# A decoder's first layer in one thread: Silu by Tanh, one block's convolution on VectorE, exponentials by tile, four product buffers

## The chip, the cores and the metric

The kernel runs on one core of one Trainium2 chip. The time is that of the device in microseconds (us), from start to end of one execution; less is better. Three runs of the kernel before gave 4592.59, 4599.94 and 4611.69 us, so the median is 4599.94. The profile is one further execution.

The engines are named as in the profile: PE is TensorE, PEld its weight loads, DVE is VectorE, ACT is ScalarE, POOL is GpSimd, SP is the queue that issues DMAs.

## The reference

A decoder of four layers, each with an attention, a cross attention and a feed-forward part, all different, works on x of 8 x 256 x 256 in float32. The change lies in the first of these twelve parts, a selective state space model in both directions. Cut to what matters:

```python
xz = xn @ W_in.T                     # 512 channels u, 512 channels z
u = silu(causal_conv4(u) + b_conv)   # depthwise, 4 taps
for d in (forward, backward):
    dt, Bm, Cm = split(u @ Wx.T)     # 64, 16, 16
    delta = softplus(dt @ Wdt.T + bdt)
    h[t] = exp(delta[t] * A) * h[t-1] + delta[t] * Bm[t] * u[t]   # 16 states
    y_d = sum over states of h[t] * Cm[t] + u * D
out = (y_f + y_b) / 2 * silu(z) @ W_out.T
```

The convolution and its Silu give u, which all else of the layer reads; Silu of z is the gate at its end; the softplus makes the deltas. Silu(v) is v times the logistic function, which is (v/2) * (tanh(v/2) + 1).

## The kernel before

**Two threads.** `build` (from L2480) runs two generators, one for blocks 0 and 1 ("left", the leading thread) and one for blocks 2 and 3 ("right"). A block is two of the eight sequences, 512 positions. Each thread goes through the twelve layers, and every `yield` adds the layer's planned time per step to the thread's clock; the thread that is earlier goes on. The right thread starts with a lag of 1.01 * FIRST = 474.7 planned units, so that the leading thread has its first layer to itself. A layer's planned time is divided by its number of steps, for this one FIRST / WIDE_STEPS = 470 / 265 (L2445). Instructions are then put in order on each engine by a scheduler that starts from this order of emission, and each engine works through its own list in order.

**The leading thread's first layer** is the class `Wide` (L723 on). It works on one block after the other, and on each in two ways, forward and backward. A way has 16 states, each of four tiles of 128 channels x 512 positions, 64 tiles in all. `way` (L782) puts out two tiles of a state, then one step of the parts that belong beside it, and so on.

**A tile** (`state`, L879): ScalarE takes Exp(delta * A) into a bank `st` of PSUM (two banks, L895), POOL multiplies `du` with a row of B that a DMA has spread over the partitions (`db`, four buffers, L897), VectorE runs the scan (L899). For three states of four the result stays in SBUF (`h`, three buffers) and `turn` (L917) transposes it on TensorE into `ht` (two banks), scales it on ScalarE with C (`ys`, L926) and transposes it back, added into y (L929). For the fourth state the result stays in `st`, VectorE multiplies it by the row of C (`hc`, two buffers, L902) and TensorE adds it to y through an identity matrix (L903).

**The parts beside the ways.** `channels` (L796) makes u: norm, transposes, W_in on TensorE, a copy to `u0` on ScalarE with three zero columns in front of each sequence (POOL's memset, L813), the convolution and Silu. In the first block the even channel groups are convolved on VectorE (L819, L821), the odd ones, and all of the next block, as four matmuls with diagonal matrices of taps on TensorE (called at L827, recorded under L395). Silu is L824 or L828. `rows` (L832) projects u to the rows of dt, B and C; `delta` (L852) makes the deltas: Abs (L862), Max (L863), after the last group Exp of -|v| (L867) and Ln (L869) over all four groups at once, sum (L872) and the product with u on POOL (L873). `gates` (L943) makes the Silu of z (L952), `gated` (L955) forms the result (L959, L962). Next block's channels, rows and deltas lie in the backward way of the first block, the second way; the gates lie in the second and the fourth.

A step that yields "ln" asks `way` to hold the next part back until the first half of a state with k % 4 == 3.

Of the kernel before, what the change touches and what calls it, by code (L numbers as in the profile page):

```python
# [8 lines left out]
F32 = mybir.dt.float32  # L9
# [713 lines left out]
class Wide:  # L723
# [8 lines left out]
    def steps(self):  # L732
        net, nc, other = self.net, self.nc, self.other
        with net.scope(y=1), other.scope(st=2, ht=2):
# [15 lines left out]
            nc.vector.tensor_tensor(self.skip, w["fD"], w["bD"], ALU.add)  # L750
            self.turning, last = None, None
# [44 lines left out]
    def channels(self, o, first=False):  # L796
# [12 lines left out]
        for c in range(4):  # L809
# [6 lines left out]
            bias = w["b_conv"][:, c : c + 1]  # L816
            if first and c % 2 == 0:
                acc = self.other.work.tile([128, 2, S], F32, name="hc", bufs=2)
                nc.vector.tensor_scalar(acc, u0[:, :, 0:S], w["conv"][:, c, 0:1], bias, ALU.mult, ALU.add)  # L819
                for k in range(1, 4):  # L820
                    nc.vector.scalar_tensor_tensor(  # L821
                        acc, u0[:, :, k : k + S], w["conv"][:, c, k : k + 1], acc, ALU.mult, ALU.add
                    )
                nc.scalar.activation(u[:, c], acc, AF.Silu)  # L824
            else:
                ps = net.bank()
                net.mms(pairs_of(ps), [(self.taps[:, c, k, :], u0[:, :, k : k + S]) for k in range(4)])  # L827
                nc.scalar.activation(u[:, c], pairs_of(ps), AF.Silu, bias=bias)  # L828
# [23 lines left out]
    def delta(self, o, d, first=False):  # L852
# [5 lines left out]
        for c in range(4):  # L858
            ps = net.bank()
            net.mms(ps, [(w[d + "Wdt"][:64, c * 128 : c * 128 + 128], o["dbc"][d][:64, :])])  # L860
            bias = w[d + "bdt"][:, c : c + 1]
            nc.scalar.activation(du[:, c, :], ps, AF.Abs, bias=bias)  # L862
            nc.vector.tensor_scalar(dl[:, c, :], ps, bias, 0.0, ALU.add, ALU.max)  # L863
            yield "ln" if c == 3 else None
        parts = [du[:, c, :] for c in range(4)] if first else [du]
        for v in parts:
            nc.scalar.activation(v, v, AF.Exp, scale=-1.0)  # L867
        for v in parts:
# [10 lines left out]
    def state(self, o, d, k, half):  # L879
# [12 lines left out]
        for c in (2 * half, 2 * half + 1):  # L892
            with self.net.tc.manual_schedule(engines={mybir.EngineType.Activation}):
# [6 lines left out]
                if not turned:  # L900
                    hc = far.tile([128, 512], F32, name="hc", bufs=2)
# [41 lines left out]
    def gates(self, o):  # L943

        net, nc, w = self.net, self.nc, self.w
        yield "ln"
        res = o["res"] = net.work.tile([128, 4, 512], F32, name="res")
        for c in range(4):
# [3 lines left out]
            nc.scalar.activation(res[:, c, :], ps, AF.Silu)  # L952
        yield

    def gated(self, o):  # L955

        net, nc, u = self.net, self.nc, o["u"]
        for c in range(4):
# [3 lines left out]
            nc.vector.scalar_tensor_tensor(u[:, c], pairs_of(o["res"][:, c, :]), 0.5, u[:, c], ALU.mult, ALU.mult)  # L962
# [1482 lines left out]
FIRST, WIDE_STEPS = 470, 265  # L2445
# [73 lines left out]
```

## Time and profile before

| what | us |
|---|---|
| median of three runs | 4599.94 |
| profiled execution | 4589.32 |
| its span | 4587.5 |
| first scan of the leading thread's first layer (L899) | 48.98 |
| its last hc (L902) | 511.4 |
| VectorE busy from 37 to 511.5 us | 373.0 |
| scans of this layer, 256 | 298.8 |
| ScalarE's Exp of this layer (L895), 256 | 172.2 |
| POOL's db of this layer (L897), 256 | 320.7 |
| table load on ScalarE, each | 1.283 |

How to read it: a row of the profile gives line, engine, operation, the tiles out<-in with their shapes and the number of instructions, then the busy time in us and the mean of one in ns, then how long the engine had been idle just before them and what ended that. A row of a table by stretches gives start and end, the length, and for each engine the busy us and the number of instructions, then the clock that TensorE was granted (1.00 is full), the busy share of the DMA engines and the GB/s. A row of waits gives who waited for whom: us in total, how often, the longest. A row in order of time gives start and length, and in brackets the idle time before it and who ended it. A float32 matmul stands as two records, one for each pass.

### The profile page before, as it was taken

How to read it: one execution, taken by the hardware profiler on the slowest of the kernel's cores; microseconds unless marked ns; L12 is line 12 of the kernel's file. 1: busy time of each engine (PE TensorE's matmuls, PEld its weight loads, DVE VectorE, ACT ScalarE, POOL GpSimd, SP SyncE). 2: the span in 40 equal slices, each digit the busy share in tenths (PEclk: the TensorE clock that was granted, in tenths of full speed). 3: DMA queues.
4: the chain of work that ended last, by engine and by line, in shares of the span. 5: the costliest groups of instructions: out<-in, count | busy, mean ns of one | idle time of the engine just before them, and what ended most of it. 6: DMA issues, size and time to landing. Idle time of an engine off the chain costs nothing.

```text
span 4587.5 us, 55922 instructions
## 1 busy us (share of the span) xinstructions
PE 3953.8 (86%) x20736; PEld 2688.3 (59%) x20736; DVE 2670.8 (58%) x5064; ACT 2028.1 (44%) x4543; POOL 1581.3 (34%) x1373
## 2 busy tenths in 40 slices
PE   6877787887787999989798998798989999978988
PEld 3545444454575767657565665555556768745755
DVE  6768778778656555461665366665474562143464
ACT  6768476677563544423232342423343342243331
POOL 5758445345544111142543233422021001132123
PEclk8999889999898999989899898777799999988999
DMA  3111233234383000017110000100010010011000
GB/s 124 57 36 51 107 92 99 80 77 112 98 266 133 1 1 1 1 45 249 47 42 1 1 33 16 43 14 1 1 49 1 15 37 1 21 41 40 2 37 19
DMA packets 96323, 239.79 MB, mean 52 GB/s; under 512 B 8395, under 2 KB 36403, under 8 KB 85683
## 3 DMA queue, kind: packets, MB, share of 16 engines
q1 hardware_dynamic: 86355, 179.49, 12.5%
q0 software_dynamic: 9696, 56.72, 3.6%
q8 instruction: 164, 2.69, 0.2%
q14 instruction: 108, 0.88, 0.1%
HBM read 216.05 MB, written 20.14 MB: 51 GB/s over the span
## 4 chain that ended last, share of the span: by engine, by line
PE 45%; DVE 13%; POOL 4%; ACT 4%; issue 3%; DMA 2%; POOLq 0%; ACTq 0%; DVEq 0%
PE mm L395 22%; PE sc L403 6%; PE sc L395 5%; PE av L403 3%; PE pt L395 3%; PE o L395 2%; PE mm L1089 2%; DVE xn L418 1%; DMA we<-in_experts,which 1%; PE mm L428 1%; PE mm L403 1%; POOL rs L416 1%; DVE hn_sq L2055 1%; DVE st L411 1%; ACT ex L1475 1%
## 5 line engine op out<-in xcount | busy, mean ns | idle before, releaser
L664 POOL TENSOR_TENSOR db<-du,rep 128x512 f32<-128x512 f32 x256 | 325.0, 1283 | 352.6 <-DVE mm L665 168.7
L665 DVE TENSOR_TENSOR_SCAN mm<-mm,db 128x512 f32<-128x512 f32 x256 | 310.2, 1223 | 92.9 <-ACT mm L662 81.8
L897 POOL TENSOR_TENSOR db<-du,rep 128x512 f32<-128x512 f32 x256 | 320.7, 1283 | 96.3 <-DVE h L899 74.3
L1461 POOL TENSOR_TENSOR qs<-q,w 128x256 f32<-128x256 f32 x256 | 157.6, 636 | 558.4 <-PE sc L395 549.9
L395 PE MATMUL mm<-xt,w 128*128 128x512 f32 (+1 forms) x704 | 302.5, 558 | 30.1 <-DVE rope_s L1412 10.3
L387 ACT COPY pv<-mm 111x384 f32<-111x384 f32 (+2 forms) x388 | 198.0, 512 | 288.9 <-PE mm L1089 128.0
L403 PE MATMUL sc<-k,q 64*128 64x333 f32 (+1 forms) x1152 | 252.3, 491 | 28.2 <-ACT pex L1066 9.8
L395 PE MATMUL sc<-k,qs 128*128 128x256 f32 x1024 | 271.8, 389 | 3.4 <-POOL x L455 1.1
L403 PE MATMUL av<-pv,v 111*64 111x256 f32 (+5 forms) x2752 | 255.2, 388 | 9.3 <-ACT pv L387 5.1
L899 DVE TENSOR_TENSOR_SCAN h<-st,db 128x512 f32<-128x512 f32 x192 | 223.2, 1208 | 43.9 <-ACT st L895 36.7
L395 PE MATMUL mm<-h,sw 128*128 128x256 f32 x1024 | 242.8, 384 | 0.0
L1089 PE MATMUL mm<-consts,pex 128*111 128x128 f32 x960 | 191.9, 310 | 38.1 <-ACT pv L387 30.9
L671 PE MATMUL y<-consts,hc 128*128 128x128 f32 x1024 | 170.9, 295 | 61.3 <-DVE hc L667 60.3
L1089 PEld LDWEIGHTS mm<-consts,pex 128*111 128x111 f32 x960 | 133.0, 185 | 150.0 <-issue 59.9
L395 PE MATMUL mm<-kv,w 128*128 128x256 f32 (+1 forms) x640 | 202.8, 439 | 20.6 <-ACT q L1031 10.4
L395 PE MATMUL mm<-w,ao 128*128 128x256 f32 x768 | 203.6, 405 | 14.2 <-DVE ao L389 5.1
L395 PEld LDWEIGHTS sc<-k,qs 128*128 128x128 f32 x1024 | 183.6, 193 | 49.7 <-issue 21.1
L395 PEld LDWEIGHTS mm<-h,sw 128*128 128x128 f32 x1024 | 192.4, 192 | 32.6 <-issue 6.7
L1475 ACT ACTIVATE ex<-sc,nm 128x256 f32<-128x256 f32 x256 | 119.5, 471 | 196.4 <-DVE nm L1471 182.1
L395 PEld LDWEIGHTS mm<-xt,w 128*128 128x128 f32 x704 | 130.4, 201 | 126.7 <-issue 74.8
L1066 ACT ACTIVATE pex<-sc,pnm 128x333 f32<-128x333 f32 x320 | 170.0, 537 | 76.7 <-DVE pnm L1061 68.5
L403 PEld LDWEIGHTS av<-pv,v 128*32 128x32 f32 (+3 forms) x2752 | 123.2, 133 | 127.9 <-issue 47.0
(484 smaller groups left out, 9098.9 us busy)
## 6 DMA issues: line engine op xcount, KB each, us to landing
rep<-rows2f SPq DMA_DIRECT2D x32, 512.0 KB, 4.8
rep<-rows2b SPq DMA_DIRECT2D x32, 512.0 KB, 4.8
rep<-rows3f SPq DMA_DIRECT2D x32, 512.0 KB, 4.8
rep<-rows3b SPq DMA_DIRECT2D x32, 512.0 KB, 5.2
w<-in_w SPq DMA_DIRECT2D x12, 1024.0 KB, 7.6
w<-in_w SPq DMA_DIRECT2D x8, 1025.0 KB, 9.1
w<-in_w SPq DMA_DIRECT2D x6, 1001.0 KB, 8.3
w<-in_w SPq DMA_DIRECT2D x6, 838.0 KB, 10.9
```

Of the source, the lines that this page charges most:

```text
L387: self.nc.scalar.copy(out, in_)
L395: self.nc.tensor.matmul(out, lhsT=lhs, rhs=rhs, start=n == 0, stop=n == len(pairs) - 1)
L403: self.nc.tensor.matmul(out, lhsT=lhs, rhs=rhs, start=start, stop=stop, tile_position=at)
L664: nc.gpsimd.tensor_tensor(db, du[:, c, :], rep[:, 0], ALU.mult)
L665: nc.vector.tensor_tensor_scan(st[:, order], st[:, order], db[:, order], 0.0, ALU.mult, ALU.add)
L671: nc.tensor.matmul(self.y[i // 2][:, at : at + 128], lhsT=hc[:, i * 128 : i * 128 + 128], rhs=net.ident, is_transpose=True, start=d == "f" ...
L897: nc.gpsimd.tensor_tensor(db, du[:, c, :], self.rep[:, 0], ALU.mult)
L899: nc.vector.tensor_tensor_scan(h[:, order], st[:, order], db[:, order], 0.0, ALU.mult, ALU.add)
L1066: self.nc.scalar.activation(self.ex[:, e, :], self.sc[:, e, :NK], AF.Exp, bias=self.nm[:, e : e + 1], accum_out=self.sm[:, e : e + 1],)
L1089: self.nc.tensor.transpose(pt[:CH, j * 128 : j * 128 + 128], ex[:, e, j * CH : (j + 1) * CH], net.ident)
L1461: nc.gpsimd.tensor_tensor(qs[:, kc].rearrange("p n (h t) -> p n h t", h=H), q[:, kc, t0 : t0 + 16].rearrange("p (n t) -> p n t", n=2).unsq ...
L1475: nc.scalar.activation(ex[:, i, :], sc[:, i * S : (i + 1) * S], AF.Exp, bias=nm[:, i : i + 1], accum_out=sm[:, i : i + 1],)
```

## The change

Silu is taken from Tanh: u becomes (Tanh(v/2) + 1) * (v/2), with v/2 from taps and bias that are halved once at the start (`half`), and the gates become (Tanh(z/2) + 1) * z, which is twice Silu, so that the factor in `gated` goes from 0.5 to 0.25. In the first block's odd groups ScalarE writes v/2 as well. All groups of the next block are convolved on VectorE. The Exp of the deltas follows each group's Abs and Max; only the Ln waits for all four. The gates no longer ask to be held back, and yield after each group. `hc` has four buffers, and the convolution two of its own (`acc`). The constant WIDE_STEPS goes from 265 to 270.

```diff
--- before.py
+++ after.py
@@ -748,6 +748,10 @@
                 nc.vector.tensor_scalar(e, e, -1.0, None, ALU.mult)
                 self.neg_a[d] = e
             nc.vector.tensor_tensor(self.skip, w["fD"], w["bD"], ALU.add)
+
+            self.half = near.tile([128, 5, 4], F32, name="half")
+            nc.vector.tensor_scalar(self.half[:, :4, :], w["conv"], 0.5, None, ALU.mult)
+            nc.vector.tensor_scalar(self.half[:, 4, :], w["b_conv"], 0.5, None, ALU.mult)
             self.turning, last = None, None
             now = {"blk": net.blks[0]}
             for part in (self.channels(now, True), self.rows(now, "f"), self.delta(now, "f", True)):
@@ -813,19 +817,21 @@
             nc.gpsimd.memset(u0[:, :, 0:3], 0.0)
             nc.scalar.copy(u0[:, :, 3:], pairs_of(ps))
             yield
-            bias = w["b_conv"][:, c : c + 1]
-            if first and c % 2 == 0:
-                acc = self.other.work.tile([128, 2, S], F32, name="hc", bufs=2)
-                nc.vector.tensor_scalar(acc, u0[:, :, 0:S], w["conv"][:, c, 0:1], bias, ALU.mult, ALU.add)
+            bias = self.half[:, 4, c : c + 1]
+            acc = near.tile([128, 2, S], F32, name="acc", bufs=2)
+            if not first or c % 2 == 0:
+                nc.vector.tensor_scalar(acc, u0[:, :, 0:S], self.half[:, c, 0:1], bias, ALU.mult, ALU.add)
                 for k in range(1, 4):
                     nc.vector.scalar_tensor_tensor(
-                        acc, u0[:, :, k : k + S], w["conv"][:, c, k : k + 1], acc, ALU.mult, ALU.add
+                        acc, u0[:, :, k : k + S], self.half[:, c, k : k + 1], acc, ALU.mult, ALU.add
                     )
-                nc.scalar.activation(u[:, c], acc, AF.Silu)
+                nc.scalar.activation(u[:, c], acc, AF.Tanh)
             else:
                 ps = net.bank()
                 net.mms(pairs_of(ps), [(self.taps[:, c, k, :], u0[:, :, k : k + S]) for k in range(4)])
-                nc.scalar.activation(u[:, c], pairs_of(ps), AF.Silu, bias=bias)
+                nc.scalar.activation(acc, pairs_of(ps), AF.Identity, scale=0.5, bias=bias)
+                nc.scalar.activation(u[:, c], pairs_of(ps), AF.Tanh, scale=0.5, bias=bias)
+            nc.vector.scalar_tensor_tensor(u[:, c], u[:, c], 1.0, acc, ALU.add, ALU.mult)
             yield
         o["dbc"], o["rows"], o["cols"], o["delta"] = {}, {}, {}, {}
 
@@ -861,11 +867,9 @@
             bias = w[d + "bdt"][:, c : c + 1]
             nc.scalar.activation(du[:, c, :], ps, AF.Abs, bias=bias)
             nc.vector.tensor_scalar(dl[:, c, :], ps, bias, 0.0, ALU.add, ALU.max)
+            nc.scalar.activation(du[:, c, :], du[:, c, :], AF.Exp, scale=-1.0)
             yield "ln" if c == 3 else None
-        parts = [du[:, c, :] for c in range(4)] if first else [du]
-        for v in parts:
-            nc.scalar.activation(v, v, AF.Exp, scale=-1.0)
-        for v in parts:
+        for v in [du[:, c, :] for c in range(4)] if first else [du]:
             nc.scalar.activation(v, v, AF.Ln, bias=1.0)
         yield
         for c in range(4):
@@ -898,7 +902,7 @@
                 h = self.hs[:, c, :] if turned else st
                 nc.vector.tensor_tensor_scan(h[:, order], st[:, order], db[:, order], 0.0, ALU.mult, ALU.add)
                 if not turned:
-                    hc = far.tile([128, 512], F32, name="hc", bufs=2)
+                    hc = far.tile([128, 512], F32, name="hc", bufs=4)
                     nc.vector.tensor_tensor(hc, st, self.rep[:, 1], ALU.mult)
                     nc.tensor.matmul(
                         self.y[c],
@@ -943,14 +947,14 @@
     def gates(self, o):
 
         net, nc, w = self.net, self.nc, self.w
-        yield "ln"
         res = o["res"] = net.work.tile([128, 4, 512], F32, name="res")
         for c in range(4):
             ps = net.bank()
             cols = slice(512 + c * 128, 640 + c * 128)
             net.mms(ps, [(w["W_in"][:, k, cols], o["xt"][:, k, :]) for k in range(2)])
-            nc.scalar.activation(res[:, c, :], ps, AF.Silu)
-        yield
+            nc.scalar.activation(res[:, c, :], ps, AF.Tanh, scale=0.5)
+            nc.vector.scalar_tensor_tensor(res[:, c, :], res[:, c, :], 1.0, ps, ALU.add, ALU.mult)
+            yield
 
     def gated(self, o):
 
@@ -959,7 +963,7 @@
             nc.vector.scalar_tensor_tensor(
                 u[:, c], u[:, c], self.skip[:, c : c + 1], pairs_of(o["y"][c]), ALU.mult, ALU.add
             )
-            nc.vector.scalar_tensor_tensor(u[:, c], pairs_of(o["res"][:, c, :]), 0.5, u[:, c], ALU.mult, ALU.mult)
+            nc.vector.scalar_tensor_tensor(u[:, c], pairs_of(o["res"][:, c, :]), 0.25, u[:, c], ALU.mult, ALU.mult)
         yield
         for b in range(2):
             net.project(o["blk"], b, u[:, :, b], self.w["W_out"])
@@ -2442,7 +2446,7 @@
 SHARE = (620, 300, 150, 300, 80, 140, 140, 120, 170, 110, 160, 100)
 
 
-FIRST, WIDE_STEPS = 470, 265
+FIRST, WIDE_STEPS = 470, 270
 
 
 def steps_of(layer, blks):
```

## Prediction

> **What bounds the kernel now.** I read the page's busy times first, then the busy times of each engine in four stretches of the changed layer, then what VectorE waits for in them, and last the order of time. The page says that TensorE is the busiest engine of the whole program:
>
> ```profile
> PE 3953.8 (86%) x20736; PEld 2688.3 (59%) x20736; DVE 2670.8 (58%) x5064; ACT 2028.1 (44%) x4543; POOL 1581.3 (34%) x1373
> ```
>
> That average says nothing about the leading thread's first layer, which runs nearly alone until 511 us. Its four ways (forward and backward for two blocks) end at 158.6, 299.5, 413.5 and 511.5 us, by the last scan of each:
>
> ```profile
> core 0: us, PE busy (x) PEld busy (x) DVE busy (x) ACT busy (x) POOL busy (x), PEclk, DMA share, GB/s
> 37.00:158.60 121.60, 89.14 (x461) 59.24 (x461) 101.11 (x115) 93.97 (x144) 96.46 (x76) 0.86 0.18 57
> 158.60:299.50 140.90, 110.44 (x517) 67.34 (x516) 91.78 (x94) 100.63 (x146) 85.19 (x71) 0.95 0.13 39
> 299.50:413.50 114.00, 83.41 (x462) 59.41 (x461) 96.27 (x106) 80.51 (x122) 85.80 (x69) 0.93 0.16 47
> 413.50:511.50 98.00, 76.62 (x433) 53.38 (x432) 83.81 (x80) 76.60 (x119) 74.79 (x63) 0.95 0.17 49
> ```
>
> VectorE is idle for 49.1 us of the second way, 17.7 of the third and 14.2 of the fourth. Undisturbed, sixteen state tiles take this:
>
> ```profile
> 391.45:413.45 22.00, 16.36 (x105) 11.63 (x104) 20.86 (x20) 17.48 (x29) 19.77 (x17) 1.00 0.20 61
> ```
>
> VectorE works 20.9 of 22.0 us there: it is the floor, 88 us for a way of 64 tiles, and POOL is close behind at 19.8. So the excess over 88 is either VectorE's other work or waiting. Its waits in the second way:
>
> ```profile
> DVE hc L902 <- PE y L903: 25.3, 3, 12.5
> DVE h L899 <- ACT st L895: 13.0, 11, 3.2
> DVE st L899 <- ACT st L895: 4.1, 5, 1.8
> DVE dl L872 <- ACT du L869: 2.6, 1, 2.6
> ```
>
> Half is one wait: the third product hc needs one of two buffers, freed by TensorE's sum into y. In order of time on VectorE, then on TensorE:
>
> ```profile
> 186.84 1.22 DVE L899 TENSOR_TENSOR_SCAN h<-st,db 128x512 f32<-128x512 f32 x1 [2.67 <-ACT st L895]
> 191.24 1.22 DVE L899 TENSOR_TENSOR_SCAN h<-st,db 128x512 f32<-128x512 f32 x1 [3.18 <-ACT st L895]
> ...
> 219.42 0.69 DVE L902 TENSOR_TENSOR hc<-st,rep 128x512 f32<-128x512 f32 x1 [10.66 <-PE y L903]
> 222.22 0.69 DVE L902 TENSOR_TENSOR hc<-st,rep 128x512 f32<-128x512 f32 x1 [2.10 <-PE y L903]
> ...
> 260.75 0.69 DVE L902 TENSOR_TENSOR hc<-st,rep 128x512 f32<-128x512 f32 x1 [12.50 <-PE y L903]
> ```
>
> ```profile
> 215.78 2.74 PE L395 MATMUL ht<-u,taps 128*128 128x512 f32 x6
> 218.37 1.02 PE L903 MATMUL y<-hc,consts 128*128 128x512 f32 x2
> ```
>
> The sum at 218.37 stands behind the next block's convolution. The waits at 186.84 and 191.24 are ScalarE changing its table for the gates' Silu and back, twice.
>
> **The change, part by part.** The sum is made against the profiled execution: 4589.3 us, of which 4587.5 are the span. The median of the three runs is 4599.9, 10.6 us more; I take the same difference off it.
>
> *Table loads.* These rows, with one shape each, price them:
>
> ```profile
> L895 ACT ACT_TABLE_LOAD x11 | 14.1, 1283 | 0.2
> L952 ACT ACT_TABLE_LOAD x4 | 5.1, 1283 | 0.1
> L872 DVE TENSOR_TENSOR dl<-dl,du 128x512 f32<-128x512 f32 x16 | 15.8, 1016 | 11.9 <-ACT du L869 10.1 <-issue 1.7
> L821 DVE SCALAR_TENSOR_TENSOR hc<-u,w,hc 128x512 f32<-128x512 f32 x6 | 4.5, 747 | 0.1
> L962 DVE SCALAR_TENSOR_TENSOR u<-res,u 128x512 f32<-128x512 f32 x8 | 5.6, 738 | 0.0
> ```
>
> The built order (how the instructions stand on each engine once the kernel is built) has 27 loads in this layer before and 11 after: 16 x 1.283 = 20.5 us of ScalarE time. What counts is what VectorE waited for them. At the gates that is 2.67 + 3.18 + 0.54 = 6.4 us in the second way and 6.4 in the fourth (the same three waits at 441, 446 and 448 us). At the convolution's Silu it is 3.08 + 1.63 at 239 and 246 us. All of it goes: 11.1 us in the second way, 6.4 in the fourth.
>
> *Four buffers and no taps.* The next block's convolution leaves TensorE: 16 instructions, by the trace 3.60 us for a channel group, 14.4 us in all. TensorE then does 110.4 - 14.4 = 96 us of the second way, and VectorE may run two products further ahead. Of 25.3 + 1.75 us (the last is the scan that follows at 263 us) I take 25 off and leave 2: the rows' projections (16 passes in some 7.5 us) still stand in that queue. Bounds: 12 if they alone set the second stall, 27.
>
> *Convolution on VectorE.* Per group one multiply (0.55, L819), three multiply-adds (0.75, L821) and one product for Silu, also 0.75: 3.55 us, 14.2 for four. Here the Trainium skill speaks against the change: by "SBUF — State Buffer", section "Who interferes with whom", a VectorE instruction with two SBUF inputs and a GpSimd one that reads SBUF exclude each other, and the later one blocks until the other is done. The 16 multiply-adds and products have two SBUF inputs, and POOL forms db from two SBUF tiles (1283 ns each) for most of the way. If each had to wait half a db it would cost 16 x 0.64 = 10.3 us more. The nearest row is L872, of the same port pattern beside the same POOL work: it has a mean of 1016 ns with its shortest at 684, so 0.33 each. I take the row: 5.3 us; bounds 0 (L962 has a mean of 738 with POOL idle or waiting) and 10.3.
>
> *New waits.* The product u <- u,acc now waits on VectorE for ScalarE's Tanh, and ScalarE's queue has transposed states in front of it that wait for TensorE. Queued behind it on VectorE are scans and hc, and behind those POOL's db. No row shows this wait; the nearest are the dl waits on ACT at L863, some 0.6 to 3.0 us. The built order puts one to four VectorE instructions between, so I take 0.7 x 4 = 2.8; bounds 0 and 8. POOL's memset of the next padded input now waits for the convolution on VectorE, with db behind it. Before, it waited 8.4 us for the taps matmuls, behind which db lay too. I take 2 us; bounds 0 and 5.
>
> *Gates.* Eight products with one input in PSUM, 0.74 each as the L959 row of that kind: 2.9 us in the second way and 2.9 in the fourth.
>
> *Exponentials by tile.* Four of 0.63 us replace one of 1.9 before the Ln: 0.6 us more of ScalarE, but none of it in one piece in front of the states. At 282 to 299 us VectorE waited 7.4 us round this place; I take 1.4 off it, and 2 off each of ways one and three (there with 3.1 us of hc waits and 5.5 of dl waits).
>
> *Start.* One load less on the chain to the first scan (1.3), two 0.75 us products more on it, partly beside other work: I take -1 in all, bounds -2 and +1. The scaled taps are two VectorE instructions of under 0.2 us, beside the first matmuls: nothing; without that cover 0.4. No DMA is added; of SP's 401 instructions 390 keep their order, so its queue costs nothing here.
>
> Sum for the second way: -11.1 -25.0 -1.4 +14.2 +5.3 +2.8 +2.0 +2.9 = -10.3. Fourth: -6.4 + 2.9 = -3.5. First and third: -4. Start: -1. Together -18.8 us. VectorE after it: 91.8 + 14.2 + 5.3 + 2.9 = 114.2 busy in a way of about 130.
>
> *Behind the layer.* Its steps now number 270, as the constant says; before they were 263 against 265. So the leading thread enters its second layer 3.5 units of planned time later (470 against 466.5), while the other thread still starts at 474.7. From there on the two mix otherwise: of all VectorE's instructions only about 70% stand in a common order. The work is equal, apart from table loads: 158 before, 153 after, and 7 fewer in the trailing thread's state loop (L662), where scans wait for ScalarE. Five are 6.4 us; I take half, -3. The rest I take as nothing. From 520 us on TensorE has 3564 of 4067 us, so 503 idle; a twentieth of that either way is 25 us, an estimate of how far another mixture may move the end.
>
> Total: -21.8, so 4578.
>
> **The rivals.** *A: as summed*, 0.45, at 4578. *B: more of it*, 0.20: the whole 27 us go, no port waits, no Tanh wait, and the later mixture is kinder by 10: -21.8 -2 -5.3 -2.8 -10 = -42, so 4558. For it speaks that TensorE has slack once the taps are gone. *C: the gain doesn't reach the end*, 0.13: VectorE becomes the bound of the second way. With port waits at 10.3, Tanh waits at 8 and the freed stall at 12, the way costs -10.3 + 5.0 + 5.2 + 13.0 = +12.9, hence +1.4 in all: 4601. Against it: POOL itself waits 96 us of the layer. *D: the mixture behind the layer*, 0.22: the trailing thread's state loop (VectorE waits 81.8 us there for ScalarE) and the attentions beside it get in each other's queues; idle TensorE time grows by a tenth, 50 us, less the 21.8: 4628. It decides from about +45 us on. For it: a third of the instructions move. Against it: the work and its steps are the same.
>
> **How the numbers follow.** A measurement tells 0.5%, 23 us: faster is below 4577, slower above 4623. A's spread is about +-12 round 4578, so a bit under half of it counts as faster (0.22) and the rest as same (0.23). B is faster; C is same, with a little to either side; D is slower for the most part. Faster 0.44, same 0.35, slower 0.21. Range: 4546 (B's lower end) to 4625, which leaves most of D out.
>
> **What would show it.** Right: 11 loads before the layer's end; the waits of hc on y gone; the second way near 130 us and the fourth near 94.5; the layer's last scan at about 492 instead of 511; from there to the end within 25 us of the 4076 of before. Wrong: the second way at 140 with multiply-adds of over 1.1 us (C); a layer that ends 20 us earlier with an end that doesn't (D); scans waiting for db behind a memset.

## The result, and the profile after

The changed kernel takes 4624.66 us (median of six runs, 4616.28 to 4627.60) where the kernel before, in the same series, takes 4606.93. The ratio on record is 1.0050, 95% interval 1.0032 to 1.0069 (the two medians alone give 1.0038): slower by about half a per cent. The forecast was 4578, faster by about half a per cent. The sign was wrong; the time lies at the upper end of the range that was given, 4546 to 4625, where rival D stood.

The profiled execution has a span of 4622.0 us against 4587.5. That is 34.5 us more, twice the 17.7 between the medians, since the profiled execution of the kernel before was 17.6 us under its median and that of the changed kernel 0.9. Runs of one kernel differ by some 40 us, the slower ones mostly at a lower clock (51 runs of the kernel before, in a later series, go from 4568.37 us at a mean clock of 0.921 to 4608.19 at 0.910), so a difference of some 10 us between two profiles says little.

The busy times of the whole program, from the page of the changed kernel, say little, and that little is strange: TensorE is busy 24.6 us longer, though it lost the 14.4 us of taps.

```profile
PE 3978.4 (86%) x20704; PEld 2697.1 (58%) x20704; DVE 2708.5 (59%) x5098; ACT 2004.5 (43%) x4533; POOL 1580.7 (34%) x1373
```

The layer itself did what it was meant to. This is the table by stretches of the changed kernel, one row for each way (they end at the last hc of each; start and end, length, then busy time and number of instructions of each engine, granted clock, DMA share, GB/s):

```profile
core 0: us, PE busy (x) PEld busy (x) DVE busy (x) ACT busy (x) POOL busy (x), PEclk, DMA share, GB/s
37.00:161.00 124.00, 92.00 (x461) 61.77 (x462) 101.13 (x115) 93.78 (x145) 95.97 (x76) 0.83 0.18 58
161.00:284.40 123.40, 91.95 (x452) 57.61 (x450) 108.81 (x119) 85.48 (x135) 89.30 (x71) 0.93 0.15 44
284.40:399.70 115.30, 82.02 (x466) 58.92 (x467) 97.45 (x106) 80.48 (x125) 86.54 (x69) 0.94 0.15 46
399.70:498.10 98.40, 74.67 (x449) 53.59 (x448) 85.58 (x84) 72.40 (x116) 75.02 (x61) 0.97 0.16 49
```

The second way fell from 140.9 to 123.4 us, and the layer's last hc stands at 498.1 instead of 511.4: 13.3 us earlier. VectorE's waits in the second way of the changed kernel (us in total, how often, the longest; its L903 is the scan, L906 hc, L928 a transpose) no longer hold hc waiting for y, which took 25.3 us, and scans wait for ScalarE's Exp for 0.5 us where it was 17.1. The longest are now:

```profile
DVE dl L869 <- ACT du L868: 5.5, 2, 3.5
DVE h L903 <- PE ht L928: 4.7, 3, 3.0
DVE hc L906 <- issue: 1.9, 1, 1.9
```

All of the loss lies behind the layer. One stretch for each kernel, from the layer's last hc to the end, first before:

```profile
511.40:4587.50 4076.10, 3570.26 (x18812) 2438.76 (x18810) 2280.93 (x4618) 1664.27 (x3996) 1234.40 (x1083) 0.92 0.16 51
```

then after:

```profile
498.10:4622.00 4123.90, 3613.61 (x18825) 2455.04 (x18823) 2296.15 (x4618) 1661.23 (x3994) 1229.27 (x1085) 0.90 0.16 50
```

It is 47.8 us longer. TensorE is busy 43.4 of these with the same matmuls (18,812 and 18,825 records), and idle 510.3 us instead of 505.8, only 4.5 more. So hardly anything queues longer: the same matmuls run slower, at a granted clock of 0.90 instead of 0.92. By the clock records TensorE had half its clock for 823 us of this stretch, before for 688; it was busy for 665 and 565 us of these. What is left when half of this busy time at half clock is taken off all busy time is an estimate of the work at full clock: 3288 us before, 3281 after. It is nearly the same, so the 43.4 us are the clock's.

Followed by landmarks (the same instruction in both traces), the changed kernel was still some 10 us ahead at 1200 us and some 3 behind from 1500 to 1950; between 2290 and 2490 us it lost some 30 more. There the two threads stand beside each other with two attentions: in the leading one, called the routed attention here, the scores are matmuls on 32 of TensorE's 128 rows (`sc<-k,q`, L403); the other mixes its heads and uses whole matmuls (`sc<-k,qs`, `pt<-mix,ex`, L395). The stretch before:

```profile
2346.00:2450.00 104.00, 102.08 (x656) 68.68 (x656) 44.21 (x94) 35.95 (x92) 25.38 (x34) 1.00 0.00 1
```

and the first part of the same attentions after:

```profile
2346.00:2357.00 11.00, 9.45 (x52) 6.08 (x44) 8.73 (x18) 0.84 (x2) 8.58 (x8) 1.00 0.01 1
2357.00:2418.00 61.00, 61.00 (x222) 34.80 (x224) 13.21 (x24) 13.06 (x28) 11.28 (x13) 0.50 0.00 0
```

For 61 us TensorE is busy all the time and has half its clock (such a stretch is called a spell from here on). At full clock these matmuls would take some 30 us, an estimate by halving. The experiments had two questions: where does the loss behind the layer come from, and what holds the clock down in such a spell?

### The profile page after: what moved, and what is told of

Same layout as the page of the kernel before. It is cut to its first block, busy times and chain, and to the rows that moved or that the text cites. A ratio compares the mean times of both kernels' runs of the same rounds, so it can differ in the third digit from the quotient of the medians.

```text
span 4622.0 us, 55781 instructions
## 1 busy us (share of the span) xinstructions
PE 3978.4 (86%) x20704; PEld 2697.1 (58%) x20704; DVE 2708.5 (59%) x5098; ACT 2004.5 (43%) x4533; POOL 1580.7 (34%) x1373
## 4 chain that ended last, share of the span: by engine, by line
PE 49%; DVE 11%; POOL 4%; ACT 3%; issue 2%; DMA 1%; POOLq 0%; ACTq 0%; DVEq 0%; SPq 0%
PE mm L395 23%; PE sc L403 7%; PE sc L395 5%; PE av L403 3%; PE o L395 3%; PE pt L395 3%; PE mm L1093 2%; DVE xn L418 1%; PE mm L428 1%; PE mm L403 1%; DMA we<-in_experts,which 1%; PE mm L1947 1%; DVE hn_sq L2059 1%; DVE st L411 1%; ACT ex L1479 1%
## 5 line engine op out<-in xcount | busy, mean ns | idle before, releaser
L395 PE MATMUL mm<-xt,w 128*128 128x512 f32 (+1 forms) x704 | 299.3, 554 | 24.5 <-DVE rope_s L1416 6.9
L403 PE MATMUL sc<-k,q 64*128 64x333 f32 (+1 forms) x1152 | 274.0, 521 | 30.9 <-ACT pex L1070 19.3
L395 PE MATMUL sc<-k,qs 128*128 128x256 f32 x1024 | 274.4, 392 | 4.4 <-POOL k L1418 2.9
L403 PE MATMUL av<-pv,v 111*64 111x256 f32 (+5 forms) x2752 | 260.3, 397 | 7.8 <-ACT pv L387 4.0
L395 PE MATMUL mm<-h,sw 128*128 128x256 f32 x1024 | 242.4, 382 | 0.0
L903 DVE TENSOR_TENSOR_SCAN h<-st,db 128x512 f32<-128x512 f32 x192 | 222.1, 1206 | 34.0 <-PE ht L928 16.4
L416 POOL TENSOR_TENSOR rs<-ve,neghalf 128x4 f32<-128x4 f32 (+1 forms) x57 | 59.3, 1041 | 465.1 <-DVE ve L414 461.5
L395 PE MATMUL mm<-kv,w 128*128 128x256 f32 (+1 forms) x640 | 202.5, 438 | 17.8 <-ACT q L1035 7.7
L395 PEld LDWEIGHTS sc<-k,qs 128*128 128x128 f32 x1024 | 184.0, 194 | 49.3 <-issue 21.9
L395 PEld LDWEIGHTS mm<-h,sw 128*128 128x128 f32 x1024 | 191.0, 191 | 32.6 <-issue 7.7
L395 PE MATMUL mm<-w,ao 128*128 128x256 f32 x768 | 198.4, 398 | 12.5 <-DVE ao L389 8.2
L933 PE MATMUL y<-consts,ys 128*128 128x128 f32 x768 | 132.3, 301 | 82.3 <-ACT ys L930 81.9
L403 PEld LDWEIGHTS av<-pv,v 128*32 128x32 f32 (+3 forms) x2752 | 125.6, 136 | 132.2 <-issue 48.7
```

What stands on the lines that cost most here:

```text
L395: self.nc.tensor.matmul(out, lhsT=lhs, rhs=rhs, start=n == 0, stop=n == len(pairs) - 1)
L403: self.nc.tensor.matmul(out, lhsT=lhs, rhs=rhs, start=start, stop=stop, tile_position=at)
L903: nc.vector.tensor_tensor_scan(h[:, order], st[:, order], db[:, order], 0.0, ALU.mult, ALU.add)
L933: nc.tensor.matmul(self.y[c][:, i * 128 : i * 128 + 128], lhsT=ys[:, c * 128 : c * 128 + 128], rhs=net.ident, is_transpose=True, start=fir ...
```

## The experiments

Lengths of ways, ends of the layer and times at half clock come from one profile each; the same first way, in kernels that don't differ in it, varied by some 4 us from profile to profile (109.4 in the kernel before, 105.2 in *b_clock*). Ratios are to the kernel before, with 95% intervals.

### Where the order behind the layer comes from

*Theory O*: the layer's gain is real, and the loss comes from the planned clock: 270 steps of 470/270 let the leading thread leave the layer at 470 planned units, where 263 steps of 470/265 had left at 466.5, and the scheduler's order of all that follows, the mixture of the two threads, differs. *The rival*: the parts themselves cost more behind the layer, or waits of their own. The constant alone can be changed in both kernels. With 272.0517 the changed kernel leaves at 466.5, and its order behind the layer is that of the kernel before; with 263 the kernel before leaves at 470 and has the order of the changed one (in both pairs over 99% of VectorE's instructions behind the layer stand in the same order).

```diff
 # a_clock: the changed kernel
-FIRST, WIDE_STEPS = 470, 270
+FIRST, WIDE_STEPS = 470, 272.0517
 # b_clock: the kernel before
-FIRST, WIDE_STEPS = 470, 265
+FIRST, WIDE_STEPS = 470, 263
```

> The changed kernel with one constant altered: 270 steps are planned as 470 / 272.05 each, so that the leading thread leaves its first layer at 466.5 planned units, as before the change. Behind the layer the built order is then that of before. Theory O (what is lost behind the layer is lost by the mixture of the two threads alone): last hc at 498 us as in the changed kernel, 4076 +- 10 us behind it as before, so a ratio to before near 0.993 to 0.995. Rival L (the loss comes from the new layer itself, because it ends earlier or leaves something behind it): the loss stays, a ratio near 1.004, with some 4124 us behind the last hc.

> The kernel before with one constant altered: WIDE_STEPS is 263, so that the leading thread leaves its first layer at 470 planned units, as in the changed kernel. Behind the layer the built order is then that of the changed kernel. O: last hc at 511 us as before, 4124 +- 10 us behind it, so a ratio near 1.006 to 1.008. L: nothing is lost, 4076 us behind it, a ratio near 1.000.

Measured: *a_clock* 0.9977 (0.9966 to 0.9989), *b_clock* 1.0100 (1.0076 to 1.0124). Both went the way of theory O, *a_clock* by less than it had (0.993 to 0.995) and *b_clock* by more (1.006 to 1.008). Behind the layer, first *a_clock*, then *b_clock*:

```profile
494.30:4573.50 4079.20, 3576.07 (x18824) 2441.97 (x18822) 2280.77 (x4617) 1667.72 (x3999) 1233.55 (x1085) 0.91 0.16 51
507.30:4619.60 4112.30, 3619.19 (x18812) 2462.57 (x18810) 2295.94 (x4618) 1661.16 (x3991) 1229.71 (x1083) 0.90 0.16 50
```

Its layer done, *a_clock* needs 3.1 us more than the kernel before; *b_clock* needs 36.2 more, without one of the change's other edits in it. It has the spell as well, at the same place:

```profile
2358.00:2419.00 61.00, 61.00 (x222) 35.03 (x218) 13.47 (x26) 13.07 (x28) 11.64 (x14) 0.50 0.00 1
```

The clock does not rest on these profiles alone. Its mean over a run was 0.901 to 0.904 in all six runs of the changed kernel and 0.897 to 0.901 in all six of *b_clock*; it was 0.914 to 0.924 in the 22 of *a_clock* and 0.910 to 0.922 in the 51 of the kernel before beside them.

That settles the first question. The order costs 0.7% (the changed kernel against *a_clock*) to 1.0% (*b_clock* against before), 36 to 48 us by the profiles. The other edits gain 0.23% in the order of before. The two don't add up exactly: +1.0 and -0.23 would be +0.77%, measured is +0.5, and only the intervals meet.

### The parts of the layer

Four kernels are *a_clock* with one part taken back (in *a_gates* the constant is 265, which with its 263 steps also leaves at 466.5), one is the kernel before with one part added.

```diff
 # a_hc2
-hc = far.tile([128, 512], F32, name="hc", bufs=4)
+hc = far.tile([128, 512], F32, name="hc", bufs=2)
 # a_taps
-            if not first or c % 2 == 0:
+            if first and c % 2 == 0:
 # a_gates: all four gates in one step, held back as before
+        yield "ln"
...
-            yield
+        yield
 # a_exp: the four Exp in one piece ahead of the Ln
-            nc.scalar.activation(du[:, c, :], du[:, c, :], AF.Exp, scale=-1.0)
-        for v in [du[:, c, :] for c in range(4)] if first else [du]:
+        parts = [du[:, c, :] for c in range(4)] if first else [du]
+        for v in parts:
+            nc.scalar.activation(v, v, AF.Exp, scale=-1.0)
+        for v in parts:
 # b_conv: the kernel before, all of the next block convolved on VectorE
-            if first and c % 2 == 0:
-                acc = self.other.work.tile([128, 2, S], F32, name="hc", bufs=2)
+            if not first or c % 2 == 0:
+                acc = near.tile([128, 2, S], F32, name="acc", bufs=2)
```

> a_clock with two hc buffers instead of four. If the four buffers carried the gain inside the layer, the waits of hc on y come back and the last hc lies at 506 to 511 us instead of 498; if taking the taps off TensorE was enough, it lies within 3 us of 498. Behind the layer as a_clock.

> a_clock with the next block's convolution back on TensorE (Silu still from Tanh, four buffers). If the move to VectorE paid, the last hc lies later than 498, by 3 to 12 us; if VectorE's 18 us of added work only cost time and the four buffers cover TensorE's queue, it lies 3 to 10 us earlier. Behind the layer as a_clock.

> a_clock with the gates put out as before the change: held back, then all four groups in one step (still from Tanh, so without table loads). If the new waits of the scan on transposes in the fourth way (3.9 and 4.8 us at 432 and 441 us of the changed kernel) come from spreading the gates over four steps, the fourth way falls from 97.4 to 90 to 93 us and the second by 2 to 5, ratio to a_clock 0.997 to 0.999; if they come from the Tanh and its product themselves, both ways stay within 2 us.

> a_clock with the deltas' Exp over all four groups at once, as before the change. If Exp by tile is what lengthened the first way (112.5 to 112.8 us against 109.4), the first way falls by 3 us or more and the third by 1 to 3; if the first way's length only moves with the spells of half clock, it stays at 110 to 113 us.

> The kernel before with one part of the change alone: the next block's convolution on VectorE (Silu, its table loads, two hc buffers, gates and Exp as before; planned clock as before, so the order behind the layer stays). If TensorE's queue was the second way's cost, that way falls from 141.2 us to 125 to 131 and the ratio is 0.997 to 0.999; if the table loads had as large a part as the prediction gave them (11 us of this way), it stays above 134.

| kernel | ratio (95%) | ways 1 to 4, us | last hc | from there to the end |
|---|---|---|---|---|
| before | 1 | 109.4, 141.2, 113.6, 98.2 | 511.4 | 4076.1 |
| after | 1.0050 (1.0032 to 1.0069) | 112.5, 123.4, 115.3, 98.5 | 498.1 | 4123.8 |
| a_clock | 0.9977 (0.9966 to 0.9989) | 112.8, 123.4, 113.2, 97.4 | 494.3 | 4079.2 |
| a_hc2 | 0.9965 (0.9953 to 0.9977) | 111.3, 130.0, 112.0, 98.2 | 500.5 | 4069.3 |
| a_taps | 1.0003 (0.9986 to 1.0020) | 111.4, 137.8, 116.5, 97.4 | 511.6 | 4088.1 |
| a_gates | 0.9984 (0.9971 to 0.9996) | 111.3, 122.3, 121.4, 94.4 | 498.5 | 4085.9 |
| a_exp | 0.9976 (0.9960 to 0.9992) | 112.9, 123.2, 118.0, 93.2 | 495.4 | 4086.9 |
| b_conv | 1.0005 (0.9991 to 1.0020) | 110.9, 131.8, 122.4, 98.2 | 513.2 | 4093.1 |

What follows. *The convolution's move* is what the second way lives on. Alone (*b_conv*) it takes 9.4 us off that way, with two buffers still: the waits of hc on y fall from 25.3 to 3.2 us there.

```profile
DVE hc L902 <- PE y L903: 3.2, 3, 1.9
```

But *b_conv* loses nearly as much in its third way, and its ratio was not the 0.997 to 0.999 expected: it gains nothing in all. Taken back (*a_taps*), the second way is 14.4 us longer, the layer ends where it did before the change, and a wait appears that neither kernel has (*a_taps*; L834 is the product for Silu, L833 the Tanh):

```profile
DVE u L834 <- ACT u L833: 23.0, 4, 8.1
```

So Silu from Tanh needs the convolution on VectorE: otherwise VectorE, in its fixed order, stands behind a TensorE convolution and a ScalarE step. *Four buffers* shorten the second way by 6.6 us (130.0 to 123.4), but the last hc of *a_hc2* at 500.5 is within 3 us of 498, and the total gains nothing: the intervals of *a_hc2* and *a_clock* overlap. *Exponentials by tile* give nothing that can be told, in the layer or in all; the first way stays at 112.9. *The gates'* split over four steps takes 8 us off the third way (121.4 to 113.2) and adds 3 to the fourth (94.4 to 97.4), which is neither of the two outcomes expected; in all, nothing that can be told. *Tanh* itself was not run alone. With *b_conv* at 131.8 us in the second way and *a_hc2* at 130.0, some 2 us are left there for Tanh, exponentials and gates together.

### The size of the constant

If the order is a matter of the constant, others might be better. These two are the changed kernel with 268 and 275, and the third joins 268 with *a_hc2*, the two best so far.

```diff
-FIRST, WIDE_STEPS = 470, 270
+FIRST, WIDE_STEPS = 470, 268     # s268; s268_hc2 also has bufs=2 for hc
+FIRST, WIDE_STEPS = 470, 275     # s275
```

> The changed kernel with WIDE_STEPS 268: the leading thread leaves its first layer at 473.5 planned units, another mixture behind it. If mixtures differ by what TensorE loses at half clock, the time behind the last hc follows 4076 + 0.3 x (half-clock time behind - 690), within 12 us; if they differ by waits in the queues, there is no such tie.

> The changed kernel with WIDE_STEPS 275: the leading thread leaves its first layer at 461.5 planned units, a third mixture. The same tie as for s268 is asked of it: time behind the last hc = 4076 + 0.3 x (half-clock time behind - 690), within 12 us, if the clock is the cause; none if it is the queues.

> The version put together from the runs: the changed kernel with WIDE_STEPS 268 (the best mixture so far) and two hc buffers instead of four. Ratio to before 0.993 to 0.997; the last hc at 496 to 501 us, and 4065 to 4075 us behind it as in s268. If the two do not add up, it lies at s268's 0.996.

Measured: *s268* 0.9959 (0.9942 to 0.9976), *s275* 1.0044 (1.0021 to 1.0067), *s268_hc2* 0.9976 (0.9963 to 0.9989). The leading thread leaves at 473.5, 461.5 and 473.5 units, after at 470, before at 466.5, so there is no trend: a neighbour of the bad order is the best one. The formula in the expectations (0.3 us for each us at half clock) missed *s268* by 15 us. It held for *s275* within 7, but by luck, for the loss there is of another kind:

```profile
496.70:4603.90 4107.20, 3577.54 (x18824) 2436.29 (x18822) 2296.07 (x4617) 1683.73 (x4009) 1241.04 (x1085) 0.91 0.16 50
```

Its TensorE is busy 1.5 us more than in *a_clock*, and idle 26.6 more. What costs is only the time at half clock in which TensorE is busy: 665 us in the changed kernel, 591 in *s275*, 574 in *s268*, 565 before. And two gains don't add: *s268_hc2*, expected at 4065 to 4075 us behind the layer, with the order of *s268* there, needs 4096.9, which is 23.1 more than *s268*; about half of it is idle time, and it has 770 us at half clock instead of 732. The same order doesn't always have the same spells.

### What holds the clock down

The longest spells at half clock with TensorE over 95% busy (in the changed kernel 61 us at 2357, 24 at 2552, 58 at 3023, 44 at 3204, 48 at 3306; before 24, 51, 27 and 38 in the same attentions) all lie where 32-row or 32-column matmuls run among larger ones; a whole one uses all 128 rows and columns. The first kernel on TensorE alone, run once, leaves out the whole decoder: independent matmuls, back to back, in streams of whole ones, of 32-row ones, of three 32-row to one whole, of 32-column ones.

> Not the decoder: a kernel of TensorE instructions alone, without waits between them, on tiles of x; it leaves out the whole computation. In this order, all float32 with 256 columns moved: 200 whole matmuls (128 rows, 128 columns of weights), 240 on 32 rows (the shape of the routed layer's scores), 160 whole, 80 times three on 32 rows and one whole, 160 whole, 240 with 32 columns of weights, 100 whole. If the clock drops because the array is little used, it goes to half in the stage of 32 rows and in the mixed one, though TensorE never idles, and comes back with the whole ones. If it drops only behind idle time, it stays at 1.00 from the first spell to the end.

```profile
13.00:430.00 417.00, 417.00 (x2821) 319.70 (x2820) 0.00 (x0) 0.00 (x0) 0.00 (x0) 1.00 0.00 1
```

The clock is 1.00 through all streams, so neither the 32-row matmuls nor the mixed stream drops a full clock. In order of time, the 32-row stream, a whole one, and the start of the mixed one:

```profile
97.19 26.18 PE L37 MATMUL bank<-t 32*128 32x256 f32 x480
123.31 69.33 PE L32 MATMUL bank<-t 128*128 128x256 f32 x320
192.57 0.71 PE L37 MATMUL bank<-t 32*128 32x256 f32 x6
193.21 0.70 PE L32 MATMUL bank<-t 128*128 128x256 f32 x2
193.84 0.71 PE L37 MATMUL bank<-t 32*128 32x256 f32 x6
```

A 32-row record takes 55 ns in its own stream, each on the next 32 rows, and a whole one 217. So the 32-row stream isn't a stream of a little-used array; the mixed one may be. Its six and two records would take 0.76 us at these rates and take 1.27 (192.57 to 193.84), though TensorE counts as busy throughout.

The second such kernel, also run once, adds idle gaps ahead of each stream, a long one of 11 to 12 us and a short one of 2.2 to 3.0:

```python
for stage in (rows, mixed, columns, whole):   # 32 rows; 3 x 32 rows + 1 whole; 32 columns
    gap(8); stage()
    gap(1); stage()
    whole(100)
```

> This kernel leaves out the whole decoder: TensorE alone runs streams of independent float32 matmuls (256 columns) as in the first such kernel, now with idle gaps ahead of them, in which TensorE waits for a chain on VectorE: a long one (some 10 to 15 us) and a short one (some 3 to 5 us) ahead of each stream. The streams, in this order, each twice: on 32 of 128 rows; three on 32 rows to one whole; on 32 columns; whole; a stream of whole ones closes each pair. The question is the spell of 61 us at half clock in the changed kernel, in which TensorE is 98% busy, mostly with matmuls on 32 rows or 32 columns. Theory K (once an idle gap has dropped the clock, matmuls that use a quarter of the array don't lift it again): after the gap the streams on 32 rows and 32 columns stay at 0.50 for all their length (some 100 us or more), the mixed one for long, and the whole one only for some 3 to 10 us; each clock comes back at the latest in the closing whole stream. Theory L (only idle time counts, whatever the matmuls use): every stream is back at 1.00 within some 3 to 10 us after its gap, the ones on 32 rows as soon as the whole ones; then the 61 us are not told by the kind of matmul.

Three stretches of it: 32-row matmuls behind the long gap, then the mixed ones with both gaps, then the whole ones that close that pair:

```profile
75.00:102.80 27.80, 27.80 (x480) 24.64 (x480) 0.13 (x1) 0.00 (x0) 0.00 (x0) 0.94 0.01 2
188.50:512.00 323.50, 320.73 (x1111) 140.53 (x1112) 2.89 (x7) 0.00 (x0) 0.00 (x0) 0.50 0.00 0
512.00:563.00 51.00, 46.52 (x210) 39.57 (x209) 4.30 (x5) 0.00 (x0) 0.00 (x0) 0.97 0.00 0
```

The 32-row stream by itself is at full clock some 3.5 us after its start, against theory K; the 32-column one is after 3.1. The mixed stream stays at 0.50 for 323 us, with TensorE busy for 320.7 of them, against theory L; the clock comes back 1.3 us after the first of the whole ones that follow. So the clock has a memory: the stream that keeps a full clock in the first kernel keeps a halved one in the second. Here the Trainium skill, "TensorE: Matmul & The Clock Gate", section "Part 1: The HAM clock gate", says that the full clock comes back after some 3.4 us of sustained activity, a matter of time and not of how many matmuls are issued. The whole, the 32-row and the 32-column streams agree; the alternating one, busy by the profile, does not. Whether it is the alternation as such or the array's lower use in it (0.76 of 1.27 us, by the estimate above) that keeps the clock down, these kernels don't separate.

Is it so in the kernel too? In order of time on TensorE, the middle of the changed kernel's spell:

```profile
2365.99 2.07 PE L403 MATMUL sc<-k,q 32*128 32x256 f32 x6
2367.99 0.90 PE L1813 MATMUL mm<-consts,top 128*128 128x128 f32 x3
2368.69 0.64 PE L395 MATMUL pt<-mix,ex 128*128 128x128 f32 x2
2369.25 1.22 PE L403 MATMUL sc<-k,q 32*128 32x256 f32 x2
```

It alternates every one or two us. In *a_clock* the clock dropped in the same attentions too, at 2334.5 us, but there 64 records of 32 columns came next, in one piece:

```profile
2335.88 6.34 PE L403 MATMUL mm<-pv,v 128*32 128x256 f32 x64
```

It was back at 2341.4, after 6.8 us. In the changed kernel, where the alternating stream followed, the drop at this place cost 61.4 us of half clock. The next two runs put this to the test; their theory K is what is left of K, that the alternating stream doesn't lift a dropped clock and whole matmuls alone do.

*a_burst* puts the four transposes of L1813 out six times over at this one place, 24 whole products in a row, into the same bank with the same values; the order is otherwise the changed kernel's but for a few neighbours. *s268_burst* does so in all eight passes of both threads' routed attentions, for the first pair of channel groups, on top of *s268*.

```diff
                     ps = net.bank()
-                    for n in range(2):
-                        for i in range(2):
-                            nc.tensor.transpose(
...
+                    times = 6 if net.side == "left" and blk is net.blks[0] and b == 0 and c == 0 else 1
+                    with net.tc.manual_schedule(engines={mybir.EngineType.PE}) if times > 1 else ExitStack():
+                        for m in range(4 * times):
+                            n, i = m % 4 // 2, m % 2
...
```

> The changed kernel with one edit far from the layer: in the leading thread's routed attention, first block, first sequence, first pair of channel groups, the four transposes of the row maxima (L1813, whole 128x128 matmuls) are put out six times over, 24 in one piece on TensorE, into the same bank with the same values. They stand some 10 us into the spell of 61 us at half clock; the order on TensorE is otherwise the changed kernel's but for a few places. Theory K (a dropped clock isn't lifted by a stream that alternates matmuls on 32 rows with whole ones, and is lifted by some 3 to 7 us of whole ones alone, as the kernel on TensorE alone shows): the clock is back at 1.00 right behind the 24 transposes, the spell that was 61 us is some 15 to 20, and the kernel gains half of the missing 40 us less the 20 added transposes (some 3 to 6 us): about -14 to -18 us against the changed kernel, so near 1.001 of the kernel before. Theory L (the spell lasts for another reason, waits or idle time of which the records show nothing): the clock stays at 0.50 through the transposes and after, and the kernel is 3 to 7 us longer than the changed one, ratio 1.006.

> The changed kernel with the constant at 268 (0.9959 of the kernel before), and the six-fold transposes for the first pair of channel groups in all eight passes of both threads' routed attentions (a sequence each). In the changed kernel five passes of these attentions had a spell of 24 to 61 us at half clock with TensorE always busy. Theory K: each pass that would be at half clock is lifted by its burst; at 40 us saved of half clock on four or so of them (20 us of time each) and 8 x 3 to 6 us for the bursts, it gains 20 to 50 us against the same kernel without bursts: 4525 to 4555, ratio 0.985 to 0.992. Theory L: it costs the bursts, 25 to 50 us: ratio 1.002 to 1.007.

*a_burst*, in order of time, then two stretches: up to the end of the transposes, and behind them:

```profile
2369.29 5.08 PE L1816 MATMUL mm<-consts,top 128*128 128x128 f32 x23
2374.29 1.13 PE L403 MATMUL sc<-k,q 32*128 32x256 f32 x6
```

```profile
2360.00:2374.00 14.00, 14.00 (x50) 9.86 (x46) 3.42 (x7) 0.00 (x0) 9.30 (x10) 0.52 0.00 1
2374.00:2406.00 32.00, 31.93 (x222) 20.12 (x220) 10.46 (x20) 13.52 (x30) 3.17 (x6) 1.00 0.00 1
```

Six 32-row records take 1.13 us behind the burst where they took 2.07; the spell is 13.7 us instead of 61.4. The kernel takes 0.9979 of the time before (0.9968 to 0.9990), so, by the two ratios to the kernel before, 20 added transposes made the changed kernel faster by 0.7%, some 33 us. Behind the layer the profile is 27.5 us shorter (4123.8 to 4096.3), more than the 14 to 18 expected: the spell's 47.7 us of half clock are worth 23.9, less about 4 for the transposes, and the rest is in other spells, which also moved (all half clock behind the layer fell by 62 us). In all 17 of its runs the mean clock was 0.906 to 0.911, in the six of the changed kernel 0.901 to 0.904. Theory K is thus shown for this spell. *s268_burst* shows it again: the spell of 61.4 us that *s268* has at this place ends during the transposes, after 10.2. Its ratio, 0.9945 (0.9925 to 0.9965), is the lowest of all here, but the gain is less than expected and not told apart from *s268* (0.9959): half clock fell from 732 to 672 us behind the layer, which is worth 30, and the added transposes cost about as much: the work at full clock rose from 3281 to 3311 us.

## Why the prediction was wrong

*What bounds the layer, and its sum.* Predicted -18.8 us by the layer's end, measured -13.3 (511.4 to 498.1), or -17.1 in *a_clock*, whose layer is the same program. The second way gained more than predicted, -17.8 for -10.3. VectorE's busy time there rose by 17.0 us, where the sum had 22.4, and its idle time fell by 34.5, where the sum had 32.7. So the term that was mis-sized is in the main the price on VectorE of the new work (changed kernel, second way, shapes kept apart):

```profile
L825 DVE SCALAR_TENSOR_TENSOR acc<-u,half,acc 128x512 f32<-128x512 f32 x12 | 11.3, 964 | 0.0
L834 DVE SCALAR_TENSOR_TENSOR u<-u,acc 128x512 f32<-128x512 f32 x4 | 3.1, 782 | 0.0
L817 POOL MEMSET u<- 128x6 f32 x2 | 0.2, 104 | 3.8 <-DVE acc L825 3.8
```

A multiply-add took 964 ns in the mean, 0.22 us over the undisturbed 747, and a product 0.04 over: 12 x 0.217 + 4 x 0.035 = 2.7 us where I had 5.3. The rows of all the new work add up to 19.1 us, of which 2 lie over neighbouring instructions. The mean hides two kinds:

```profile
204.07 1.16 DVE L825 SCALAR_TENSOR_TENSOR acc<-u,half,acc 128x512 f32<-128x512 f32 x1
205.61 2.73 DVE L825 SCALAR_TENSOR_TENSOR acc<-u,half,acc 128x512 f32<-128x512 f32 x4
209.98 1.75 DVE L825 SCALAR_TENSOR_TENSOR acc<-u,half,acc 128x512 f32<-128x512 f32 x1
```

Five of the twelve ran with no POOL instruction beside them, in 739 to 741 ns. Of the seven others three took 721 to 724 and four 1156 to 1753. That fits the exclusion which the prediction took from the Trainium skill, "SBUF — State Buffer", section "Who interferes with whom": either no wait or a long one. The bound of 10.3 us had every one of sixteen wait for half a db; only four multiply-adds waited long.

The Tanh waits (2.8) don't appear among VectorE's waits at all. POOL's memset waits 3.8 us for the convolution where it waited 8.4 for the taps, so the 2 us added there were none. The waits that were to go did go, with 11 table loads in the layer as the built order said, but others came in their place: 4.7 us of scans on transposes, and 5.5 us of dl on ScalarE where 2.6 had been. The order of causes is by *b_conv* and *a_hc2*: TensorE's relief first, buffers second.

*Fourth, first and third way.* Predicted -3.5 and -4, measured +0.3 and +4.8; in *a_clock* and its four variants the third and fourth together take 210 to 216 us where they took 211.8. The table loads did go, but scans then waited for the transposes instead. From the third way on, first before, then the changed kernel:

```profile
DVE h L899 <- ACT st L895: 17.4, 24, 3.2
DVE h L903 <- PE ht L928: 11.7, 5, 4.8
```

Of the first way, 3 us of difference lie within what one program shows from profile to profile, and *a_exp* doesn't shorten it.

*Behind the layer: the step that failed.* "The rest I take as nothing", with an estimate of 25 us either way. It is +47.8 us, the order alone (*b_clock*) +36.2. I had seen that about 30% of VectorE's instructions leave the common order, and priced that at nothing since the work was equal. Two things were missed. The shift was no part of what the edits do in the layer: the gates' steps made 270 of 263, the constant was set to match, and it could be taken out again, as *a_clock* shows. And equal work was not equal time where TensorE carries the stretch: how long its clock stayed halved depended on what stood next to what (61.4 us against 13.7 in *a_burst*). Rival D had the place and the size (4628 forecast, 4624.66 measured), but the wrong mechanism: it had TensorE's idle time growing by a tenth through queues, and idle time grew by 4.5 us, busy time by 43.4. So the size that D got right was luck; only *s275* loses chiefly by idle time.

*The five table loads fewer behind the layer* (-3): after has 153 there as predicted, and *s268* 148, *s275* 168; beside the spells nothing of this size can be read.

*Still open.* It is not known what drops the clock at such a place. In the changed kernel TensorE had idled 1.55 us just before; in *a_burst* 0.78 and 0.56; before, with gaps of 0.56, 0.29 and 0.15 us, the same attentions kept 1.00. In the second kernel on TensorE alone gaps of 2.8 and 3.0 us dropped it and one of 2.2 did not. *s268* has the spell of 61 us too (gaps of 1.14 and 0.29) and takes less time all the same, by fewer or shorter spells elsewhere. So the bursts show what ends a spell, not where the next one starts, and which order is good was found by trying.

## What to carry to other kernels

Before a change to one stage is priced, ask whether it shifts the order of all later ones; here a step count did, by 0.7 to 1.0%, three to four times what the other edits were worth. Hold that order fixed while the edits are judged, and choose it afterwards. Where one engine carries the stretch, compare its busy time for equal work between two traces: if that grew and its idle time didn't, look at the clock, not at the queues.

## What the runs showed of the hardware that I had not expected

- TensorE's clock, once halved, stays halved while 32-row and whole matmuls alternate: 323 us in the kernel on TensorE alone, 61 us in the decoder, both with TensorE 99 to 100% busy. The same stream leaves a full clock at full (1.00 in the first kernel on TensorE alone).
- It came back within 3.5 us in a stream of one kind (whole, 32-row or 32-column), and by the end of 5.1 us of 128x128 transposes. In the changed kernel three dips ahead of the long spell (at 2295.7, 2326.4 and 2336.7 us) lasted 3.4 us each; the fourth, met by the alternating stream, 61.4.
- Twenty superfluous transposes, some 4 us of work, shortened the kernel by some 33 us.
- A VectorE multiply-add of two SBUF tiles either ran undisturbed beside POOL (721 to 724 ns) or took 1156 to 1753 ns.
